# A two-layer attention and state-space kernel: scans and products of two groups in one instruction, with the preparation spread over two images

## The chip, the cores and the metric

The kernel runs on one core of one Trainium2 chip. The metric is the time of one execution in device microseconds (us). In the profile PE is TensorE's matmuls and PEld its weight loads, DVE is VectorE, ACT is ScalarE, POOL is GpSimd and SP is SyncE, whose queue issues the DMAs.

## The reference

The input is a batch of 128 images of 128 channels and 32 x 32 = 1024 pixels, fp32. The first layer is attention with four heads over the batch axis, once per pixel, with a residual and a layernorm over channels; the change doesn't touch it. The second layer has a convolution branch and a state-space branch (`_mamba`), image by image. Cut to what matters:

```python
xh = einsum('oi,bihw->bohw', cv1_w, x) + cv1_b
l = silu(batchnorm(depthwise_conv3x3(xh)))
t = layernorm(xh over channels) * ln_g + ln_b          # 1024 tokens x 128
xm, z = split(t @ in_proj_w.T)                         # 256 each
xm = silu(causal_conv1d(xm, 4 taps) + conv1d_b)
dt, Bm, Cm = split(xm @ x_proj_w.T)                    # 8, 16, 16
dt = softplus(dt @ dt_proj_w.T + dt_proj_b)
dA = exp(dt[..., None] * A)                            # 256 channels x 16 states
dBu = dt[..., None] * Bm * xm[..., None]
h = dA_t * h + dBu_t                                   # over the 1024 tokens
y = sum over states of h * C_t, plus xm * D
g = (y * silu(z)) @ out_proj_w.T
out = x + cv2(concat(l, g))
```

So each image has 256 x 16 = 4096 recurrences of 1024 steps, each with a factor (the decay dA) and an addend (the input dBu), and each result is multiplied by C and summed over the 16 states.

## The kernel before, in words

`attention_layer` writes the first layer's result to `mid` in DRAM. `mamba_layer` then takes one image per `step`.

The 4096 recurrences are cut into NG = 32 groups of 128 partitions (32 channels x 4 states); `place(k)` gives a group's half h of the channels, block nb of states and block db of channels. Per group:

- SP broadcasts dt (`dtr`) and dt times xm (`dtxr`) over the states, and B (`brep`) and C (`crep`) over the channels, from DRAM (L730, L733).
- `ahead` lets ACT compute the decay `da` (L756) and POOL the input `dbu` (L759), two groups before they are used (AHEAD).
- `group` lets DVE scan (L765) and multiply by C (L767). `da` has two buffers in PSUM, and the scan writes back into them, except in the groups of `on_pool` (6 of 32), whose scan goes to `hc` in SBUF and whose product POOL makes (`product`, L772).
- `sums` lets PE add up the states of four groups into `y_ps` (L788), and `gate` multiplies by silu(z) on DVE (L797).

While the groups of one image run, the instructions that prepare the next one (`prologue`: projections, layernorm, the 1d and 2d convolutions, dt and its product, their stores to DRAM) and those that finish the previous one (`outputs`) are issued between them. `spread` is the planner. It gives every group a slot of SLOT = 3.4 us, charges each engine what the groups use of it (`busy`), and puts each `Op`, with its cost and dependences, into the first slot where its engine has time and one of two PSUM banks is free. The order of the instructions on each engine is then fixed by the program's text: in slot k come `group(k)`, `ahead(k + 2)`, `product(k)`, loads, `sums`, `gate`, and the planned ops. The engines run their own queues in order and wait for one another.

The layernorm is four steps per half of an image: ACT centres (`centred`, L534) and squares (L537), PE averages the squares, ACT makes the reciprocal root (`rstd`, L549 and L550), POOL multiplies (`normed`, L555), and ACT applies ln_g and ln_b (`affine`, L560) into `tn`, which the four taps (`xm_mm`, L586) and z's projection (L702) read.

Images 1 to 124 run in a hardware loop, four images a pass; the others are written out before and behind it.

Of the kernel before, what the change touches and what calls it, by code (L numbers as in the profile page):

```python
# [40 lines left out]
NDB = P // GD  # L41
NG = DI2 * NNB * NDB
AHEAD = 2
# [271 lines left out]
SLOT = 3.4  # L315


def spread(ops, busy, banks, slots):
# [5 lines left out]
    for s in range(slots):  # L324
# [3 lines left out]
        while again:  # L328
            again = False
            for op in left:  # L330
# [3 lines left out]
                for d in op.deps:  # L334
                    at = max(at, ends[d] + (0.0 if d.eng == op.eng else 0.3))
# [23 lines left out]
def mamba_layer(ctx: ExitStack, tc: tile.TileContext, ident, eps, mid, w, out):  # L359
# [73 lines left out]

    wk = const.tile([P, DC, DI2 * P], F32, name="wk")
    wfT = const.tile([P, DI2, P], F32, name="wfT")
    b1c = const.tile([P, 1], F32, name="b1c")
    with tc.tile_pool(name="b_prep", bufs=1) as prep, tc.tile_pool(
# [15 lines left out]
        for h in range(DI2):  # L453
            wf_ps = prep_ps.tile([P, P], F32, name=f"wf_ps{h}")
            nc.tensor.matmul(
                wf_ps, lhsT=opw[:, h * P : (h + 1) * P], rhs=cv2gT, start=True, stop=True
            )
            nc.vector.tensor_copy(wfT[:, h, :], wf_ps)
        b_ps = prep_ps.tile([P, 1], F32, name="b_ps")
# [23 lines left out]
    dtr = several(NDB, [P, L], "dtr")  # L483
    dtxr = several(NDB, [P, L], "dtxr")
    brep = several(NNB, [P, L], "brep")
    crep = several(NNB, [P, L], "crep")
    dbu = several(4, [P, L], "dbu")
    hc = several(8, [P, L], "hc")
# [3 lines left out]
    xc = several(NCH, [P, CH], "xc")  # L492
    sq = several(NCH, [P, CH], "sq")
    dt = several(DI2, [P, L], "dt")
    sp = several(DI2, [P, L], "sp")
    o = keep.tile([P, CH], F32, name="o")
    da = several(2, [P, L], "da", psum)
    y_ps = psum.tile([P, L], F32, name="y_ps")
    banks = several(2, [P, CH], "p_ps", psum)
    xp = [t[0:NX] for t in xc]  # L500

    nc.gpsimd.memset(xpad, 0.0)
# [5 lines left out]
    def prologue(b, im):  # L508
# [9 lines left out]

        def project(wT, c):
            bank = Bank()  # L520

            def mm():
                nc.tensor.matmul(bank.tile, lhsT=wT, rhs=x[:, chunk(c)], start=True, stop=True)

            reads.append(op("PE", 0.9, mm, take=bank))
            return bank, reads[-1]

        reads, writes = [], []
        tns, xhs = [], []
        for c in range(NCH):  # L530
            bank, mm = project(w1cT, c)

            def centred(c=c, bank=bank):
                nc.scalar.activation(xc[c], bank.tile, AF.Identity, bias=b1c)  # L534
# [4 lines left out]
            e1 = op("ACT", 0.7, centred, [mm])  # L539
            e2 = op("ACT", 0.7, squared, [e1], free=bank)  # L540
# [5 lines left out]
            mm = op("PE", 0.9, variance, [e2], take=var)  # L546
# [5 lines left out]
            e3 = op("ACT", 1.4, rstd, [mm], free=var)  # L552

            def normed(c=c):
                nc.gpsimd.tensor_mul(xc[c], xc[c], sq[c])  # L555

            e4 = op("POOL", 1.4, normed, [e3])

            def affine(c=c):
                nc.scalar.activation(  # L560
                    tn[:, chunk(c, DC - 1)], xc[c], AF.Identity, bias=lnb, scale=lng
                )

            tns.append(op("ACT", 0.7, affine, [e4]))
        for c in range(NCH):
# [10 lines left out]
            xhs.append(op("ACT", 0.7, padded, [mm], free=bank))  # L576
# [3 lines left out]
        for c in range(NCH):  # L580
            for h in range(DI2):
                bank = Bank()

                def xm_mm(c=c, h=h, bank=bank):
                    for k in range(DC):
# [5 lines left out]
                            stop=k == DC - 1,  # L591
# [5 lines left out]
                late = op("PE", 3.5, xm_mm, tns[: c + 1], take=bank)  # L597
                pre.append(op("ACT", 0.6, xm_copy, [late], free=bank))
# [8 lines left out]
        silu = op("ACT", 4.9, xm_silu, pre)  # L607
# [25 lines left out]

        for h in range(DI2):
            done = []
            for c in range(NCH):
# [11 lines left out]
                def split(c=c, h=h, bank=bank):  # L648
                    bias = dtb[:, h : h + 1]
                    nc.scalar.activation(sp[h][:, chunk(c)], bank.tile, AF.Abs, bias=bias)  # L650
                    nc.scalar.activation(dt[h][:, chunk(c)], bank.tile, AF.Relu, bias=bias)  # L651

                mm = op("PE", 0.9, a_mm, [xps[c]], take=bank)
                done.append(op("ACT", 1.4, split, [mm], free=bank))

            def log1p(h=h):
                nc.scalar.activation(sp[h], sp[h], AF.Exp, scale=-1.0)
                nc.scalar.activation(sp[h], sp[h], AF.Ln, bias=1.0)  # L658

            def dt_sum(h=h):  # L660
                nc.gpsimd.tensor_add(dt[h], dt[h], sp[h])  # L661

            def dtx_mul(h=h):
                nc.gpsimd.tensor_mul(sp[h], dt[h], im["xm"][h])  # L664

            ln = op("ACT", 2.2, log1p, done)
            add = op("POOL", 2.4, dt_sum, [ln])
            op("SP", 4.0, lambda h=h: nc.sync.dma_start(im["dt"][h], dt[h]), [add])
            mul = op("POOL", 2.4, dtx_mul, [add])
            op("SP", 4.0, lambda h=h: nc.sync.dma_start(im["dtx"][h], sp[h]), [mul])  # L670
        pre = []

        for c in range(NCH):
            bank = Bank()
            last = [*xhs, late]
            for dy in range(3):
# [13 lines left out]
                if dy == 0:  # L690
                    writes += last
# [5 lines left out]
        for c in range(NCH):  # L697
            for h in range(DI2):
# [14 lines left out]
                writes.append(op("PE", 0.9, z_mm, [tns[c], late], take=bank))  # L713
                pre.append(op("ACT", 0.6, z_copy, writes[-1:], free=bank))


        def gate_silus():
            nc.scalar.activation(im["l"], im["l"], AF.Silu, bias=bnt, scale=bns)
            for h in range(DI2):
                nc.scalar.activation(im["sz"][h], im["sz"][h], AF.Silu)  # L720
            nc.scalar.preload_act_table_set("natural_log_exp_and_others")

        op("ACT", 6.0, gate_silus, pre)
        return ops, reads, writes
# [10 lines left out]
    def load_channels(im, h, db):  # L735
        rs = slice(db * GD, (db + 1) * GD)
        by_channel(dtr[db], im["dt"][h][rs])
        by_channel(dtxr[db], im["dtx"][h][rs])
# [7 lines left out]
    def place(k):  # L746
        return k // (NNB * NDB), k // NDB % NNB, k % NDB

    def on_pool(k):
        _, nb, db = place(k)  # L750
        return db == 0 and nb < NNB - 1

    def ahead(k):

        h, nb, db = place(k)
        nc.scalar.activation(  # L756
            da[k % 2], dtr[db], AF.Exp, scale=aneg[:, h * NDB + db, nb : nb + 1]
        )
        nc.gpsimd.tensor_mul(dbu[k % 4], dtxr[db], brep[nb])  # L759

    def group(k):

        h, nb, db = place(k)
        dst = hc[k % 8] if on_pool(k) else da[k % 2]
        nc.vector.tensor_tensor_scan(dst, da[k % 2], dbu[k % 4], 0.0, ALU.mult, ALU.add)  # L765
        if not on_pool(k):
            nc.vector.tensor_mul(hc[k % 8], da[k % 2], crep[nb])  # L767

    def product(k):
        if on_pool(k):  # L770
            _, nb, _ = place(k)
            nc.gpsimd.tensor_mul(hc[k % 8], hc[k % 8], crep[nb])  # L772

    def sums(im, j):
# [11 lines left out]
        for c in range(NCH):  # L786
            for db in range(NDB):
# [3 lines left out]
                    rhs=hc[(j * NDB + db) % 8][:, chunk(c)],  # L791
# [7 lines left out]
    def outputs(b, im, reads=()):  # L799


        again = Op("SP", 4.0, lambda: load_x(b), reads, first=4)
        ops = [again]
        for c in range(NCH):
# [18 lines left out]
            mm = Op("PE", 3.5, o_mm, [again], take=bank)  # L823
# [12 lines left out]
    def end(b, im):  # L836

        return {
            0: lambda: sums(im, 2 * NNB - 1),
            2: lambda: gate(im, 1),  # L840
        }

    def step(b, im, nxt, was, then=None):


        ops, reads, writes, ending = [], [], [], {}
        if nxt is not None:
            ops, reads, writes = prologue(*nxt)
        if was is not None:
            more = outputs(*was, reads)  # L850
            reads = [op for op in more if op.eng == "PE"]
            for op in writes:
                op.deps += tuple(reads)
            ops += more
            ending = end(*was)
        if then is not None:
            ops.append(Op("SP", 4.0, lambda: load_x(then), reads))
        busy = {
            "PE": [2.4 if k % 4 == 0 else 0.0 for k in range(NG)],
            "ACT": [1.15] * NG,  # L860
# [139 lines left out]
```

## Time and profile before

| | before |
|---|---|
| median of 3 runs | 17832.34 us (17829.78 to 17835.11) |
| the profiled execution's own time | 17833.07 us |
| its span | 17831.3 us |
| instructions | 183455 |
| granted TensorE clock, mean of the span | 0.884 |
| busy: PE, DVE, POOL, ACT | 78%, 87%, 75%, 61% of the span |
| first scan of the second layer starts at | 2955.24 us |
| DMA | 2242.49 MB, mean 126 GB/s |

A line of the page's groups gives the line of the code, the engine, the operation, the names of output and inputs (buffer numbers left out), their shape, the count, the busy time with the mean duration in ns, and the idle time of the engine just before such instructions with what ended most of it. The row of 40 digits shows an engine's busy share in tenths in 40 equal slices of the span, here 446 us each. In the view of waits a line is: who waited, for whom, the total in us, how often, and the longest. In the timeline it is the start, the duration, the instruction, and in brackets the idle time ahead of it.

### The profile page before, as it was taken

What the parts mean: (1) busy time and instruction counts of PE and PEld (TensorE: products, weight loads), DVE (VectorE), ACT (ScalarE), POOL (GpSimd) and SP (SyncE); (2) the same over time, 40 slices, a digit from 0 to 9 for tenths busy, and PEclk for the clock granted to TensorE, in tenths of its full rate; (3) what the DMA queues carried; (4) which work ended last, traced back from release to release, by engine and by line L of the source; (5) the groups of instructions that cost most, each with busy time, mean ns of one, the idle gap of its engine ahead of it and who ended that gap; (6) DMA issues with size and microseconds to landing.
All of it is one profiled execution on the core that took longest, in us unless ns stands there. A gap on an engine that the chain in (4) does not pass through costs nothing. (4 is left out here: it accounts for less than half of the span.)

```text
span 17831.3 us, 183455 instructions
## 1 busy us (share of the span) xinstructions
PE 13935.2 (78%) x66058; PEld 5323.4 (30%) x66058; DVE 15497.4 (87%) x10016; ACT 10805.1 (61%) x12932; POOL 13369.2 (75%) x6152
## 2 busy tenths in 40 slices
PE   9999997777777777777777777777777777777776
PEld 6666663222222222222222222222222222222221
DVE  6777776889988989998889998999998989999898
ACT  6666665556655556655556655565655565656555
POOL 1222224888888888888888888888888888888887
PEclk9999998888888888888888888888888888888888
DMA  3222222443343443343343344343334343334343
GB/s 59 49 49 47 50 39 87 145 143 137 141 144 138 144 144 136 142 144 141 140 144 138 140 144 143 139 144 140 139 143 144 138 146 143 136 141 147 140 142 122
DMA packets 1133729, 2242.49 MB, mean 126 GB/s; under 512 B 599496, under 2 KB 600528, under 8 KB 1133136
## 3 DMA queue, kind: packets, MB, share of 16 engines
q1 hardware_dynamic: 1133136, 2233.11, 37.2%
q8 instruction: 551, 9.03, 0.2%
q14 instruction: 42, 0.34, 0.0%
HBM read 1813.40 MB, written 419.43 MB: 125 GB/s over the span
## 5 line engine op out<-in xcount | busy, mean ns | idle before, releaser
L759 POOL TENSOR_TENSOR dbu<-dtxr,brep 128x1024 f32<-128x1024 f32 x4096 | 9576.6, 2363 | 1492.3 <-DMA dtxr<-dtxd 886.1
L765 DVE TENSOR_TENSOR_SCAN da<-da,dbu 128x1024 f32<-128x1024 f32 x3328 | 7610.8, 2287 | 931.7 <-ACT da L756 917.4
L756 ACT ACTIVATE da<-dtr,aneg 128x1024 f32<-128x1024 f32 x4096 | 4555.9, 1116 | 4913.7 <-DVE hc L767 4256.9
L788 PE MATMUL y_ps<-hc,fold 128*32 128x512 f32 x16384 | 3315.2, 695 | 2593.1 <-DVE hc L767 1792.3
L767 DVE TENSOR_TENSOR hc<-da,crep 128x1024 f32<-128x1024 f32 x3328 | 4073.9, 1224 | 260.1
L681 PE MATMUL p_ps<-xpad,dwd 128*128 128x512 f32 x4608 | 2432.5, 674 | 175.8 <-ACT dt L651 175.8
L788 PEld LDWEIGHTS y_ps<-hc,fold 128*32 128x32 f32 x16384 | 574.7, 117 | 5125.7 <-DVE hc L767 2779.4
L772 POOL TENSOR_TENSOR hc<-hc,crep 128x1024 f32<-128x1024 f32 x768 | 1812.8, 2360 | 328.7 <-DVE hc L765 205.5
L765 DVE TENSOR_TENSOR_SCAN hc<-da,dbu 128x1024 f32<-128x1024 f32 x768 | 1749.0, 2277 | 325.8 <-PEq L915 245.8
L242 POOL TENSOR_SCALAR yt<-z,nw,nb 128x512 f32<-128x512 f32 x256 | 319.7, 1249 | 2236.3 <-PE m_ps L176 1888.5
L586 PE MATMUL p_ps<-tn,wk 128*128 128x512 f32 x4096 | 1858.3, 601 | 126.2 <-ACT tn L560 126.1
L681 PEld LDWEIGHTS p_ps<-xpad,dwd 128*128 128x128 f32 x4608 | 927.1, 210 | 1606.4 <-issue 1323.1
L586 PEld LDWEIGHTS p_ps<-tn,wk 128*128 128x128 f32 x4096 | 745.6, 189 | 1229.4 <-issue 802.3
L640 PE MATMUL p_ps<-xc,dtwT 8*128 8x512 f32 x1024 | 582.1, 648 | 234.4 <-ACT xc L623 210.1
L614 PE MATMUL p_ps<-xm,xpT 128*40 128x512 f32 x1024 | 489.7, 601 | 283.7 <-ACT xc L623 234.9
L201 DVE TENSOR_TENSOR oT<-m_ps,rden 128x512 f32<-128x512 f32 x256 | 177.2, 692 | 587.4 <-ACT rden L200 587.4
L595 ACT COPY xm<-p_ps 128x512 f32<-128x512 f32 x512 | 299.6, 585 | 614.6 <-PE p_ps L586 614.6
L154 DVE TENSOR_TENSOR e<-s_ps,top 128x1024 f32<-128x1024 f32 x512 | 624.5, 1220 | 9.8 <-issue 1.1
L661 POOL TENSOR_TENSOR dt<-dt,sp 128x1024 f32<-128x1024 f32 x256 | 603.0, 2356 | 35.6 <-ACT sp L658 35.6
L150 DVE TENSOR_REDUCE top<-s_ps 128x8 f32<-128x1024 f32 x512 | 621.9, 1215 | 0.0
L664 POOL TENSOR_TENSOR sp<-dt,xm 128x1024 f32<-128x1024 f32 x256 | 603.9, 2359 | 0.2
L176 PE MATMUL m_ps<-ident,e 128*128 128x128 f32 x4096 | 579.0, 280 | 2.5 <-DVE v L238 1.8
(115 smaller groups left out, 16769.9 us busy)
## 6 DMA issues: line engine op xcount, KB each, us to landing
dtr<-dtd SPq DMA_DIRECT2D x1024, 512.0 KB, 4.6
dtxr<-dtxd SPq DMA_DIRECT2D x1024, 512.0 KB, 5.5
brep<-bcd SPq DMA_DIRECT2D x512, 512.0 KB, 4.7
crep<-bcd SPq DMA_DIRECT2D x512, 512.0 KB, 6.1
x<-mid SPq DMA_DIRECT2D x256, 512.0 KB, 4.2
dtd<-dt SPq DMA_DIRECT2D x256, 512.0 KB, 6.6
dtxd<-sp SPq DMA_DIRECT2D x256, 512.0 KB, 3.2
xt<-in_x SPq DMA_DIRECT2D x64, 1024.0 KB, 12.2
```

Source lines behind the costliest of these rows:

```text
L150: nc.vector.tensor_reduce(tops[half], s_ps[:, :, ls, :], AX.X, ALU.max)
L154: nc.vector.tensor_tensor(es[g % 2][:, :, ls, :], s_ps[:, :, ls, :], tops[half].unsqueeze(3).to_broadcast([P, NH, LG // 2, NB]), ALU.subtract,
L586: nc.tensor.matmul(bank.tile, lhsT=wk[:, k, h * P : (h + 1) * P], rhs=tn[:, c * CH + k : (c + 1) * CH + k], start=k == 0, stop=k == DC - 1,)
L661: nc.gpsimd.tensor_add(dt[h], dt[h], sp[h])
L664: nc.gpsimd.tensor_mul(sp[h], dt[h], im["xm"][h])
L681: nc.tensor.matmul(bank.tile.rearrange("p (r q) -> p r q", q=HH), lhsT=dwd[:, k, :], rhs=xpad[:, c * rows + dy : (c + 1) * rows + dy, dx : ...
L756: nc.scalar.activation(da[k % 2], dtr[db], AF.Exp, scale=aneg[:, h * NDB + db, nb : nb + 1])
L759: nc.gpsimd.tensor_mul(dbu[k % 4], dtxr[db], brep[nb])
L765: nc.vector.tensor_tensor_scan(dst, da[k % 2], dbu[k % 4], 0.0, ALU.mult, ALU.add)
L767: nc.vector.tensor_mul(hc[k % 8], da[k % 2], crep[nb])
L772: nc.gpsimd.tensor_mul(hc[k % 8], hc[k % 8], crep[nb])
L788: nc.tensor.matmul(y_ps[db * GD : (db + 1) * GD, chunk(c)], lhsT=fold, rhs=hc[(j * NDB + db) % 8][:, chunk(c)], start=False, stop=nb == NN ...
```

## The change

All of it is in the second layer.

- Groups go in pairs. NP = 16 pairs of two channel blocks, each a tile of 128 x 2 x 1024. One DVE scan covers 2048 elements; the first decay of the second half is set to 0 once, and ACT never writes it, so that the recurrence starts anew there. ACT still makes two decays of 1024 per pair (`decays`); POOL makes one input of 2048 (`inputs`); the product is one instruction of 2048 on DVE, or on POOL where `j % 4 == 2`.
- The scan always writes `hc` in SBUF and the product works in place in `hc`. `da` has one pair buffer in PSUM (even pairs) and one in SBUF (odd pairs). `dbu` has two pair buffers, `hc` four. `dt` and `sp` are single, `xc` is gone.
- The layernorm's ln_g is multiplied into `wk` and `inzT` once, ln_b goes into `convb`, `zb` and a correction of the first three columns (`corr`). `centred` and `affine` are gone; `normed` is a DVE instruction that reads the bank.
- `prologue` is cut in two: `first_part` (layernorm and the padded copy) of the image after next runs in the second half of a step, `second_part` of the next image in the step after it. Silus are held to slots 1 and 15 or later.
- SLOT is 3.16; the planner has a DVE op wait 3.0 us behind what it depends on.
- A pass of the loop has 12 images: images 1 to 120; 121 to 127 are written out.

```diff
@@ -39,8 +39,8 @@
 GD = 32
 NNB = DS // GN
 NDB = P // GD
+NTB = L // P
 NG = DI2 * NNB * NDB
-AHEAD = 2
...
-SLOT = 3.4
+SLOT = 3.16
+PASS = 12
+NP = NG // 2
...
-                    at = max(at, ends[d] + (0.0 if d.eng == op.eng else 0.3))
+                    wait = 0.0 if d.eng == op.eng else 3.0 if op.eng == "DVE" else 0.3
+                    at = max(at, ends[d] + wait)
...
+    corr = const.tile([P, DI2, DC - 1], F32, name="corr")
+    zb = const.tile([P, DI2], F32, name="zb")
...
+        for h in range(DI2):
+            o_ps = prep_ps.tile([P, DC + 1], F32, name=f"o_ps{h}")
+            for t in range(DC):
+                for k in range(DC - t):
+                    nc.tensor.matmul(
+                        o_ps[:, t : t + 1],
+                        lhsT=wk[:, k, h * P : (h + 1) * P],
+                        rhs=lnb,
+                        start=k == 0,
+                        stop=k == DC - t - 1,
+                    )
+            nc.tensor.matmul(
+                o_ps[:, DC : DC + 1],
+                lhsT=inzT[:, h * P : (h + 1) * P],
+                rhs=lnb,
+                start=True,
+                stop=True,
+            )
+            nc.vector.tensor_add(convb[:, h : h + 1], convb[:, h : h + 1], o_ps[:, 0:1])
+            nc.vector.tensor_scalar_mul(corr[:, h, :], o_ps[:, 1:DC], -1.0)
+            nc.vector.tensor_copy(zb[:, h : h + 1], o_ps[:, DC : DC + 1])
+        nc.vector.tensor_scalar_mul(wk, wk, lng)
+        nc.vector.tensor_scalar_mul(inzT, inzT, lng)
...
-    dtr = several(NDB, [P, L], "dtr")
-    dtxr = several(NDB, [P, L], "dtxr")
+
+    dtr = several(NDB // 2, [P, 2, L], "dtr")
+    dtxr = several(NDB // 2, [P, 2, L], "dtxr")
     brep = several(NNB, [P, L], "brep")
     crep = several(NNB, [P, L], "crep")
-    dbu = several(4, [P, L], "dbu")
-    hc = several(8, [P, L], "hc")
+    dbu = several(2, [P, 2, L], "dbu")
+    hc = several(4, [P, 2, L], "hc")
...
-    xc = several(NCH, [P, CH], "xc")
     sq = several(NCH, [P, CH], "sq")
-    dt = several(DI2, [P, L], "dt")
-    sp = several(DI2, [P, L], "sp")
+    dt = keep.tile([P, L], F32, name="dt")
+    sp = keep.tile([P, L], F32, name="sp")
     o = keep.tile([P, CH], F32, name="o")
-    da = several(2, [P, L], "da", psum)
+    da = several(1, [P, 2, L], "da_ps", psum) + several(1, [P, 2, L], "da")
     y_ps = psum.tile([P, L], F32, name="y_ps")
     banks = several(2, [P, CH], "p_ps", psum)
-    xp = [t[0:NX] for t in xc]
...
+    xp = several(NCH, [NX, CH], "xp")
+
+    for t in da:
+        nc.vector.memset(t[:, 1, 0:1], 0.0)
...
-    def prologue(b, im):
+    def first_part(im, after=(), start=0):
...
+            e1 = op("ACT", 0.7, squared, [mm])
             var = Bank()
 
             def variance(c=c, bank=var):
                 nc.tensor.matmul(bank.tile, lhsT=mean, rhs=sq[c], start=True, stop=True)
 
-            mm = op("PE", 0.9, variance, [e2], take=var)
+            mm = op("PE", 0.9, variance, [e1], take=var)
 
             def rstd(c=c, bank=var):
                 nc.scalar.activation(sq[c], bank.tile, AF.Ln, bias=eps)
                 nc.scalar.activation(sq[c], sq[c], AF.Exp, scale=-0.5)
 
-            e3 = op("ACT", 1.4, rstd, [mm], free=var)
-
-            def normed(c=c):
-                nc.gpsimd.tensor_mul(xc[c], xc[c], sq[c])
-
-            e4 = op("POOL", 1.4, normed, [e3])
-
-            def affine(c=c):
-                nc.scalar.activation(
-                    tn[:, chunk(c, DC - 1)], xc[c], AF.Identity, bias=lnb, scale=lng
+            e2 = op("ACT", 1.4, rstd, [mm], free=var)
+
+            def normed(c=c, bank=bank):
+                nc.vector.scalar_tensor_tensor(
+                    tn[:, chunk(c, DC - 1)], bank.tile, b1c, sq[c], ALU.add, ALU.mult
                 )
 
-            tns.append(op("ACT", 0.7, affine, [e4]))
+            tns.append(op("DVE", 0.75, normed, [e2], free=bank))
...
+    def second_part(im, written=(), silus=(0, 0)):
...
-                            stop=k == DC - 1,
+                            stop=c > 0 and k == DC - 1,
+                        )
+                    if c == 0:
+                        nc.tensor.matmul(
+                            bank.tile[:, 0 : DC - 1],
+                            lhsT=ident,
+                            rhs=corr[:, h, :],
+                            start=False,
+                            stop=True,
                         )
...
-    def place(k):
-        return k // (NNB * NDB), k // NDB % NNB, k % NDB
-
-    def on_pool(k):
-        _, nb, db = place(k)
-        return db == 0 and nb < NNB - 1
-
-    def ahead(k):
-
-        h, nb, db = place(k)
-        nc.scalar.activation(
-            da[k % 2], dtr[db], AF.Exp, scale=aneg[:, h * NDB + db, nb : nb + 1]
+    def place(j):
+
+        return j // (2 * NNB), j // 2 % NNB, j % 2
+
+    def on_pool(j):
+        return j % 4 == 2
+
+    def both(t):
+
+        return t.unsqueeze(1).to_broadcast([P, 2, L])
+
+    def flat(t):
+        return t.rearrange("p k l -> p (k l)")
+
+    def decays(j):
+
+
+        h, nb, q = place(j)
+        for i in range(2):
+            k = h * NDB + 2 * q + i
+            nc.scalar.activation(
+                da[j % 2][:, i, i:], dtr[q][:, i, i:], AF.Exp, scale=aneg[:, k, nb : nb + 1]
+            )
+
+    def inputs(j):
+        _, nb, q = place(j)
+        nc.gpsimd.tensor_mul(dbu[j % 2], dtxr[q], both(brep[nb]))
+
+    def scan(j):
+
+        nc.vector.tensor_tensor_scan(
+            flat(hc[j % 4]), flat(da[j % 2]), flat(dbu[j % 2]), 0.0, ALU.mult, ALU.add
         )
-        nc.gpsimd.tensor_mul(dbu[k % 4], dtxr[db], brep[nb])
-
-    def group(k):
-
-        h, nb, db = place(k)
-        dst = hc[k % 8] if on_pool(k) else da[k % 2]
-        nc.vector.tensor_tensor_scan(dst, da[k % 2], dbu[k % 4], 0.0, ALU.mult, ALU.add)
-        if not on_pool(k):
-            nc.vector.tensor_mul(hc[k % 8], da[k % 2], crep[nb])
-
-    def product(k):
-        if on_pool(k):
-            _, nb, _ = place(k)
-            nc.gpsimd.tensor_mul(hc[k % 8], hc[k % 8], crep[nb])
+
+    def product(j):
+        _, nb, _ = place(j)
+        eng = nc.gpsimd if on_pool(j) else nc.vector
+        eng.tensor_mul(hc[j % 4], hc[j % 4], both(crep[nb]))
...
-                    rhs=hc[(j * NDB + db) % 8][:, chunk(c)],
+                    rhs=hc[(2 * j + db // 2) % 4][:, db % 2, chunk(c)],
...
-        again = Op("SP", 4.0, lambda: load_x(b), reads, first=4)
+    def outputs(b, im):
+
+        again = Op("SP", 4.0, lambda: load_x(b), first=1)
...
-            0: lambda: sums(im, 2 * NNB - 1),
-            2: lambda: gate(im, 1),
+            1: lambda: sums(im, 2 * NNB - 1),
+            3: lambda: gate(im, 1),
...
+    SILUS = (1, 15)
+
+    def step(b, im, nxt=None, was=None, then=None):
...
+        if was is not None:
+            ops += outputs(*was)
+            ending = end(was[1])
+        xs = [op for op in ops if op.eng == "PE"]
         if nxt is not None:
-            ops, reads, writes = prologue(*nxt)
-        if was is not None:
-            more = outputs(*was, reads)
-            reads = [op for op in more if op.eng == "PE"]
-            for op in writes:
-                op.deps += tuple(reads)
+            more, reads = second_part(nxt, xs, SILUS)
             ops += more
-            ending = end(*was)
         if then is not None:
-            ops.append(Op("SP", 4.0, lambda: load_x(then), reads))
+            ops.append(Op("SP", 4.0, lambda: load_x(then), xs))
+            reads.append(ops[-1])
+            ops += first_part(im, reads, NG // 2 + 2)
...
-            "PE": [2.4 if k % 4 == 0 else 0.0 for k in range(NG)],
-            "ACT": [1.15] * NG,
-            "POOL": [4.8 if on_pool(k) else 2.4 for k in range(NG)],
+            "PE": [2.4 if k % 4 == 1 else 0.0 for k in range(NG)],
+            "ACT": [0.0, 2.3] * (NG // 2),
+            "POOL": [k % 2 * 4.5 * (1 + on_pool(k // 2)) for k in range(NG)],
...
-                group(k)
-                a = k + AHEAD
-                if a < NG:
-                    ahead(a)
-                elif nxt is not None:
-                    ahead(a - NG)
-                product(k)
-                h, nb, db = place(a % NG)
-                if nb == NNB - 1 and a < NG:
-                    if h == 0:
-                        load_channels(im, 1, db)
-                    elif nxt is not None:
-                        load_channels(nxt[1], 0, db)
-                if nxt is not None:
-                    if k == 25:
-                        load_b(nxt[1], 0)
-                        load_c(nxt[1], 0)
-                    if k == 30:
-                        load_b(nxt[1], 1)
-                    if k == 31:
-                        load_c(nxt[1], 1)
-                if k in (2, 6):
-                    load_b(im, 2 + k // 4)
-                if k in (3, 7):
-                    load_c(im, 2 + k // 4)
+                j = k // 2
+                if k % 2 == 0:
+                    scan(j)
+                else:
+                    a = j + 2
+                    h, nb, q = place(a % NP)
+                    src = im if a < NP else nxt
+                    if src is not None:
+                        decays(a % NP)
+                        inputs(a % NP)
+                        if nb == NNB - 1 and (h == 0 or nxt is not None):
+                            for do in load_dt, load_dtx:
+                                for db in 2 * q, 2 * q + 1:
+                                    do(im if h == 0 else nxt, 1 - h, db)
+                    product(j)
+                for src, do, slots in (
+                    (im, load_b, {1: 3}),
+                    (im, load_c, {3: 2, 5: 3}),
+                    (nxt, load_b, {18: 0, 21: 1, 24: 2}),
+                    (nxt, load_c, {22: 0, 30: 1}),
+                ):
+                    if k in slots and src is not None:
+                        do(src, slots[k])
+                if k % 4 == 1 and k > 1:
+                    sums(im, k // 4 - 1)
                 if k in ending:
                     ending[k]()
-                if k % NDB == 0 and k > 0:
-                    sums(im, k // NDB - 1)
-                if k == NG // 2 + 2:
+                if k == NG // 2 + 3:
...
-    step(0, a, (1, b), None, 2)
-    with tc.For_i(1, NB - 3, 4) as i:
-        for j in range(0, 4, 2):
-            step(i + j, b, (i + j + 1, a), (i + j - 1, a), i + j + 2)
-            step(i + j + 1, a, (i + j + 2, b), (i + j, b), i + j + 3)
+    step(0, a, b, None, 2)
+    with tc.For_i(1, NB - 7, PASS) as i:
+        for j in range(0, PASS, 2):
+            step(i + j, b, a, (i + j - 1, a), i + j + 2)
+            step(i + j + 1, a, b, (i + j, b), i + j + 3)
...
```

## The prediction

> **What bounds the kernel now.** I read the page's busy shares and 40 slices first, then its groups of instructions.
>
> ```profile
> PE 13935.2 (78%) x66058; PEld 5323.4 (30%) x66058; DVE 15497.4 (87%) x10016; ACT 10805.1 (61%) x12932; POOL 13369.2 (75%) x6152
> ...
> DVE  6777776889988989998889998999998989999898
> ...
> POOL 1222224888888888888888888888888888888887
> ...
> L759 POOL TENSOR_TENSOR dbu<-dtxr,brep 128x1024 f32<-128x1024 f32 x4096 | 9576.6, 2363 | 1492.3 <-DMA dtxr<-dtxd 886.1
> L765 DVE TENSOR_TENSOR_SCAN da<-da,dbu 128x1024 f32<-128x1024 f32 x3328 | 7610.8, 2287 | 931.7 <-ACT da L756 917.4
> ...
> L767 DVE TENSOR_TENSOR hc<-da,crep 128x1024 f32<-128x1024 f32 x3328 | 4073.9, 1224 | 260.1
> ```
>
> The 75% and 87% of the first line mix two stages. From slice 7 on the second layer runs, with POOL at 8 tenths and DVE at 8 to 9: DVE sets its pace and POOL has little to spare. Next I asked what DVE waited for between 4000 and 17700 us, some 118 images.
>
> ```profile
> DVE da L765 <- ACT da L756: 844.4, 385, 4.3
> DVE hc L765 <- PEq L915: 238.2, 29, 9.6
> DVE da L765 <- POOL dbu L759: 12.3, 3, 4.6
> ```
>
> Per image that is 7.2 us for ScalarE's decays (which stand behind table loads and silus in its queue), 2.0 us for the loop's end, which comes once in four images, and almost nothing for POOL. Last, in order of time, DVE and POOL side by side:
>
> ```profile
> 10066.04 2.27 DVE L765 TENSOR_TENSOR_SCAN da<-da,dbu 128x1024 f32<-128x1024 f32 x1
> 10066.25 2.36 POOL L772 TENSOR_TENSOR hc<-hc,crep 128x1024 f32<-128x1024 f32 x1 [0.83 <-issue]
> 10068.34 1.23 DVE L767 TENSOR_TENSOR hc<-da,crep 128x1024 f32<-128x1024 f32 x1
> 10068.56 4.68 POOL L759 TENSOR_TENSOR dbu<-dtxr,brep 128x1024 f32<-128x1024 f32 x2
> ```
>
> The engines overlap at full speed. The code shows what these DVE instructions share: da lies in PSUM, so every scan and product of the kernel before reads one operand from PSUM and only one from SBUF. The sole large exception is a multiplication in the preparation, during which POOL is idle:
>
> ```profile
> L446 DVE TENSOR_TENSOR wk<-wk,inxT 128x1024 f32<-128x1024 f32 x1 | 1.2, 1226 | 4.2 <-DMA wk<-in_conv1d_wT 4.2
> ```
>
> Two SBUF operands cost DVE nothing by themselves (1226 against 1224 ns). Beside a working POOL this trace never shows them.
>
> **The time to start from.** The profiled execution took 17833.07 us, its span 17831.3; the median shown is 17832.34, so the three are interchangeable. The first scan starts at 2955.24 (timeline); from there, 14876 us / 128 = 116.2 us per image. The first layer is untouched. So new time = 17831.3 + 128 x (new us per image - 116.2).
>
> [...] The trace has 1272 ns for 512 (L555) and 2363 for 1024: 1091 per 512, hence 4545 for 2048[...].
>
> **The change, part by part.** Durations of the double instructions: a product is 692 ns at 512 (L201) and 1224 at 1024, so 532 per 512 and a fixed 160; at 2048 it is 2.29 us. A scan is 2 x 2287 - 160 = 4.41 us.
>
> 1. *Pairs.* Per image 32 scans become 16 and 26 products on DVE become 12. Starts, not durations, add up: today scan to product 2.30 to 2.39 and product to next scan 1.14. DVE before: 26 x 3.49 + 6 x 2.2 + two gates at 1.13 = 106.2; with the waits above 115.4, near 116.2. DVE after: 16 x 4.46 + 12 x 2.20 + 2.3, and two new normed instructions at 0.7 = 101.4. So at full speed the pairs save 4.8 us, most of it since one product in four, not 6 in 32, goes to POOL.
> 2. *POOL.* 20 instructions at 4.50 = 90.0 (16 inputs, 4 products) and four of dt and dtx at 2.36 = 9.4: 99.4 us. Before: 38 x 2.36 + 9.4 + 2.5 of normed = 101.6.
> 3. *Where operands lie.* The scan now writes hc in SBUF, and the product reads hc and crep: two SBUF operands in all 12. The da of odd pairs is in SBUF, and dbu too: 8 scans of 16. That is 8 x 4.41 + 12 x 2.29 = 62.8 us of DVE work[...]. Before, it was zero. This part decides. Its price lies between nothing and full exclusion; I take full exclusion[...] and the trace shows why the case did not arise.
> 4. *Decays.* Freed by the scan of two pairs earlier, they have one scan and up to two products (4.4 + 2.3 + 2.3 = 9.0 us) for 2.2 us of work, enough for a silu group (two loads at 1.28 and two activations at 1.1: 4.8 us). The 7.2 us of waits should go; what is late next is POOL's inputs, which have the same 9.0 us for 4.5, or for 9.0 where a product stands in front of them.
> 5. *Layernorm folded.* ScalarE loses 2 x 0.68 + 2 x 0.80 = 3.0 us, POOL 2.5, DVE gains 1.4 (in item 1), PE gets two matmuls of three columns (0.3 us at most each, in PE's free 22%). Setup gets some 20 small matmuls, about 10 us once. Nothing here is on the path except DVE's 1.4.
> 6. *Preparation over two images.* The same instructions and the same DMAs move (per image 8 dt, 8 dtx, 8 b and c, 2 x, 4 stores), on queues with room: SP's transfers take 40% of the DMA engines. They land in 4 to 7 us and are issued two pairs, some 13 us, before use; before, POOL waited 814 us in all for dtxr. I price this at 0, and at 2 us per image if they come late. The new DVE wait, normed on ScalarE's rstd, has the next scan queued behind it; the planner puts it 3 us late. 0 to 1 us.
> 7. *Twelve images a pass.* 31 loop ends become 10: from 238/118 = 2.0 us per image to about 0.8; I use 1.0.
>
> **The sum for full exclusion.** [...]99.4 + 62.8 = 162.2 us per image; the 8 scans from PSUM (35.3 us), gates and normed hide beside POOL. Going through four pairs: a locked scan waits for POOL's inputs, POOL's next inputs wait until that scan frees one of two dbu buffers[...]. With the loop 1.0: 165.2, or 17831 + 128 x 49.0 = 24100 us. Between 160.5 (starts a little closer than durations: 23500) and 170 (0.1 us for each of some 40 hand-overs: 24700).
>
> **The rivals.**
> *Sharing without a lock.* [...]2048 x 1.04 ns = 2.13 us, for 20 instructions 42.6; with POOL's 99.4 it makes 142, or 21300 us. If only the products contend (a scan needs its operands half as fast), 99.4 + 27.5 + 1 = 128: 19300 us.[...]
> *No contention: faster.* If DVE's second SBUF read is not in POOL's way at all, DVE sets the pace with 101.4, POOL at 99.4 is nearly as long and two dbu buffers tie them closely, for which I add 4 to 5 us; with the loop 107 us, or 16650 (16150 at 102.5 without any coupling, 17200 at 111). For it: nothing in the trace has been seen to contend. Against: the trace holds no test[...]. It decides below a quarter: once more than 116.2 - 1 - 99.4 = 15.8 of the 62.8 us exclude POOL, the gain is gone.
> *No effect within 0.2%* (36 us, about what a measurement of this kernel tells from no change) needs gain and contention to cancel to 0.3 us per image.
>
> **Chances.** Full exclusion 0.42, partial 0.16, none 0.39, cancelling 0.02, otherwise slower 0.01. Likeliest is 24100, by itself 23400 to 24700. Since "none" holds more than 2 in 10, the range runs from 16250 to 24700. Faster 0.39, same 0.02, slower 0.59.
>
> **What would show it.** Right: in the second layer POOL and DVE busy times that no longer overlap for L-lines of products and odd scans; products well over 2.29 us, or starting only as POOL's inputs end; odd scans slower or later than even ones of the same size; per image near 165 us. Wrong: odd and even scans both at 4.4 us, products at 2.3 beside a POOL at 4.5, and DVE busy over 95% of each slice. A step between 125 and 145 us points to sharing. Waits of DVE for ScalarE's decays should be near zero in all cases; if they remain, item 4 is wrong.

## The result, and the profile after

| | before | after |
|---|---|---|
| median | 17833.17 us (17829.78 to 17835.11, 4 runs) | 23335.07 us (23334.36 to 23335.38, 4 runs) |
| span of the profiled execution | 17831.3 us | 23333.6 us |
| first scan of the second layer | 2955.24 us | 2977.31 us |
| per image from there (span less first scan, / 128) | 116.2 us | 159.0 us |
| busy DVE, POOL | 87%, 75% | 95%, 84% |

The ratio is 1.3085, 95% interval 1.3063 to 1.3108: slower by 31%. The first layer is as it was. The page of the changed kernel, the same parts as were shown of before:

```profile
PE 14726.9 (63%) x66614; PEld 5612.4 (24%) x66614; DVE 22202.8 (95%) x6442; ACT 10518.5 (45%) x12420; POOL 19500.3 (84%) x3592
...
DVE  7777689999999999999999999999999999999999
...
POOL 1222189999999999999999999999999999999998
...
L819 POOL TENSOR_TENSOR dbu<-dtxr,brep 128x2048 f32<-128x2048 f32 x2048 | 13687.0, 6693 | 1440.2 <-DVE hc L823 1284.7
L830 DVE TENSOR_TENSOR hc<-hc,crep 128x2048 f32<-128x2048 f32 x1536 | 8463.9, 5510 | 52.9
L823 DVE TENSOR_TENSOR_SCAN hc<-da,dbu 128x2048 f32<-128x2048 f32 x1024 | 6828.8, 6669 | 25.3 <-POOL dbu L819 17.7
...
L823 DVE TENSOR_TENSOR_SCAN hc<-da_ps,dbu 128x2048 f32<-128x2048 f32 x1024 | 4514.9, 4409 | 153.9 <-PEq L981 134.6
```

DVE issues 36% fewer instructions and is busy for 43% longer. The last two lines are the same instruction of the same size, in equal number: with the decays in PSUM (`da_ps`, even pairs) it takes 4409 ns, with the decays in SBUF (`da`, odd pairs) 6669. The product takes 5510 ns where 2.29 us were expected, POOL's input 6693 where 4.50 were. And DVE almost never waits, by the view of its waits from 4000 us to 23200:

```profile
DVE hc L823 <- PEq L981: 134.6, 9, 15.0
DVE hc L823 <- issue: 13.9, 1, 13.9
DVE hc L823 <- POOL dbu L819: 8.8, 1, 8.8
```

The 7 us per image of waits for decays are gone, as planned, and no other wait of DVE has taken their place. (POOL waits 1197 us in the same stretch for scans to free its buffers.) DVE's time is inside its instructions. The timeline of DVE and POOL (start, duration) shows how:

```profile
9995.85 4.39 DVE L823 TENSOR_TENSOR_SCAN hc<-da,dbu 128x2048 f32<-128x2048 f32 x1
9996.00 8.56 POOL L819 TENSOR_TENSOR dbu<-dtxr,brep 128x2048 f32<-128x2048 f32 x1 [1.18 <-DVE hc L823]
10000.27 6.44 DVE L830 TENSOR_TENSOR hc<-hc,crep 128x2048 f32<-128x2048 f32 x1
...
10004.52 6.56 POOL L830 TENSOR_TENSOR hc<-hc,crep 128x2048 f32<-128x2048 f32 x1
10006.64 4.41 DVE L823 TENSOR_TENSOR_SCAN hc<-da_ps,dbu 128x2048 f32<-128x2048 f32 x1
...
10011.05 11.04 POOL L819 TENSOR_TENSOR dbu<-dtxr,brep 128x2048 f32<-128x2048 f32 x2
10011.08 6.66 DVE L830 TENSOR_TENSOR hc<-hc,crep 128x2048 f32<-128x2048 f32 x1
```

The odd scan comes first and runs at its own 4.39 us. POOL's input, issued 0.15 us later, ends after 8.56: it stood still until the scan was nearly over, and ended 4.3 us after it. The product, issued meanwhile, ends 2.2 us after that input, POOL's product 4.4 us after the DVE product. In these lines one of the two engines stands while DVE has an instruction with two SBUF inputs and POOL a multiplication; only the scan from PSUM (10006.64, 4.41 us) runs beside POOL undisturbed. The last two lines start together (x2: two instructions in one line).

From such lines one gets how long each keeps the other out. The product of the last line ends after 6.66 us, so the POOL input kept it out for 6.66 - 2.29 = 4.4 us. POOL's own instruction is 4.53 us where nothing is in its way, so the scan at 9995.85 kept it out for 4.2 us from its start (0.15 + 8.56 - 4.53), and products, in other such lines, for 2.15. In the trace of the second layer there are 1028 meetings of these three kinds in which the first instruction runs at its own length and the second starts within 1 us of it. In all of them the second is blocked, each kind for nearly the same time (4.36 to 4.42, 4.20 to 4.27, 2.15 to 2.19 us). Per image 20 x 4.4 (16 inputs, and 4 products of the same size) + 4 x 2.2 (dt and dtx) + 8 x 4.2 + 12 x 2.15 = 156 us, of 159.0 measured. I call this sum the held time. Laid along the trace from 4000 to 22000 us, it leaves some 3 us per image in which nobody holds anything, which makes up the rest.

### The profile page after: what moved, and what is told of

Read it like the earlier page. It is cut to its first block, busy times and chain, and to the rows that moved or that the text cites. A ratio compares the mean times of both kernels' runs of the same rounds, so it can differ in the third digit from the quotient of the medians.

```text
span 23333.6 us, 172625 instructions
## 1 busy us (share of the span) xinstructions
PE 14726.9 (63%) x66614; PEld 5612.4 (24%) x66614; DVE 22202.8 (95%) x6442; ACT 10518.5 (45%) x12420; POOL 19500.3 (84%) x3592
## 5 line engine op out<-in xcount | busy, mean ns | idle before, releaser
L819 POOL TENSOR_TENSOR dbu<-dtxr,brep 128x2048 f32<-128x2048 f32 x2048 | 13687.0, 6693 | 1440.2 <-DVE hc L823 1284.7
L830 DVE TENSOR_TENSOR hc<-hc,crep 128x2048 f32<-128x2048 f32 x1536 | 8463.9, 5510 | 52.9
L823 DVE TENSOR_TENSOR_SCAN hc<-da,dbu 128x2048 f32<-128x2048 f32 x1024 | 6828.8, 6669 | 25.3 <-POOL dbu L819 17.7
L813 ACT ACTIVATE da<-dtr,aneg 128x1024 f32<-128x1024 f32 (+1 forms) x2048 | 2239.6, 1141 | 5794.2 <-DVE hc L823 5792.4
L823 DVE TENSOR_TENSOR_SCAN hc<-da_ps,dbu 128x2048 f32<-128x2048 f32 x1024 | 4514.9, 4409 | 153.9 <-PEq L981 134.6
L813 ACT ACTIVATE da_ps<-dtr,aneg 128x1024 f32<-128x1024 f32 (+1 forms) x2048 | 2287.8, 1117 | 3101.3 <-DVE hc L823 3051.6
L846 PE MATMUL y_ps<-hc,fold 128*32 128x512 f32 x16384 | 2662.3, 779 | 1352.0 <-POOL hc L830 1314.6
L830 POOL TENSOR_TENSOR hc<-hc,crep 128x2048 f32<-128x2048 f32 x512 | 3361.4, 6565 | 0.0
L682 PE MATMUL p_ps<-xp,dtwT 8*128 8x512 f32 x1024 | 750.5, 821 | 863.4 <-ACT dt L693 768.6
L837 PE MATMUL y_ps<-xm,skipd 128*128 128x512 f32 x1024 | 783.1, 908 | 110.0 <-DVE sz L855 110.0
```

What stands on the lines that cost most here:

```text
L682: nc.tensor.matmul(bank.tile, lhsT=dtwT[XD:NX, h * P : (h + 1) * P], rhs=xp[c][XD:NX], start=True, stop=True,)
L813: nc.scalar.activation(da[j % 2][:, i, i:], dtr[q][:, i, i:], AF.Exp, scale=aneg[:, k, nb : nb + 1])
L819: nc.gpsimd.tensor_mul(dbu[j % 2], dtxr[q], both(brep[nb]))
L823: nc.vector.tensor_tensor_scan(flat(hc[j % 4]), flat(da[j % 2]), flat(dbu[j % 2]), 0.0, ALU.mult, ALU.add)
L830: eng.tensor_mul(hc[j % 4], hc[j % 4], both(crep[nb]))
L837: nc.tensor.matmul(y_ps[:, chunk(c)], lhsT=skipd[:, h, :], rhs=im["xm"][h][:, chunk(c)], start=True, stop=False,)
```

## The experiments

The theory: a DVE instruction with two SBUF operands and a reading POOL instruction exclude each other, whole instruction against whole instruction, and the held time is the bound. The rivals: operands in SBUF are slow by themselves; the pairs, with two input buffers, couple the engines too closely; the folded layernorm and the spread preparation cost the time. Runs given below without a ratio were timed once.

**POOL only writes.** The inputs are left out of the computation; POOL fills their buffer instead.

```diff
-        nc.gpsimd.tensor_mul(dbu[j % 2], dtxr[q], both(brep[nb]))
+        nc.gpsimd.memset(dbu[j % 2], 0.5)
+        nc.gpsimd.memset(dbu[j % 2], 0.25)
+        nc.gpsimd.memset(dbu[j % 2][:, 0, :], 0.5)
```

> The changed kernel, with POOL's 16 input products per image replaced by three memsets into the same buffer (2048, 2048 and 1024 elements), so that POOL is about as long at work but only writes there; the inputs are left out of the computation. Exclusion of POOL's reads: only POOL's 4 products and 4 dt and dtx instructions per image still read, 27 us, against 62.8 us of DVE instructions with two SBUF operands; DVE sets the pace with about 101 us plus at most 4 x 4.4 us, so 103 to 118 us per image, 16200 to 18100 us in all, odd scans mostly at 4.4 us and products mostly at 2.3 us. Rival 'SBUF operands are slow by themselves': products stay at 5.5 us and odd scans at 6.7 us in the mean, total above 22500. Rival 'two input buffers couple the engines too closely': the order and the buffers are unchanged, so the total stays above 21000.

Measured: 18283 us, 119.6 us per image. The groups of instructions:

```profile
L825 DVE TENSOR_TENSOR_SCAN hc<-da,dbu 128x2048 f32<-128x2048 f32 x1024 | 5040.8, 4923 | 1662.7 <-POOL dbu L821 1617.1 <-PE y_ps L848 29.8 <-PE p_ps L570 9.4
...
L832 DVE TENSOR_TENSOR hc<-hc,crep 128x2048 f32<-128x2048 f32 x1536 | 3524.3, 2294 | 52.6
L832 POOL TENSOR_TENSOR hc<-hc,crep 128x2048 f32<-128x2048 f32 x512 | 3245.7, 6339 | 2.0 <-DVE hc L825 2.0
```

The product with the same operands in SBUF is back at 2294 ns: SBUF operands aren't slow by themselves, that rival falls. POOL writes for 4.6 us per pair beside it (memsets of 1804, 1804 and 951 ns), and neither is lengthened. But the total is a little above my upper end of 18100: DVE now waits for POOL's buffers (1617 us in all, 12.6 us per image). That is the coupling, and it is looked at below.

**Four products per image from PSUM.**

```diff
-            flat(hc[j % 4]), flat(da[j % 2]), flat(dbu[j % 2]), 0.0, ALU.mult, ALU.add
+            flat(da[0] if j % 4 == 0 else hc[j % 4]),
+            flat(da[j % 2]),
+            flat(dbu[j % 2]),
...
-        eng.tensor_mul(hc[j % 4], hc[j % 4], both(crep[nb]))
+        src = da[0] if j % 4 == 0 else hc[j % 4]
+        eng.tensor_mul(hc[j % 4], src, both(crep[nb]))
...
```

These products stand ahead of the decays, and a memset of one column restores the 0 at the seam.

> The changed kernel, but the four scans per image with j % 4 == 0 write back into the PSUM buffer, so that their four products on DVE read one operand from PSUM; the decays that follow wait for the product. Exclusion: the held time falls by 4 x 2.29 = 9.2 us per image, from 159 to about 150, so 22150 us (21900 to 22500), these four products at 2.3 us and the other eight and the odd scans still lengthened. 'Slow by themselves': the four products fall from 5.5 to 2.3 us, 13 us per image less, about 21700. 'Coupling': no gain or a loss, since the decays wait longer: 23300 or more.

Measured: 22294 us, ratio to before 1.2511 (1.2475 to 1.2547), 150.9 us per image: 8.1 us less than the changed kernel, where the held time is 8.6 to 9.2 less. The two kinds of product in one kernel:

```profile
L836 DVE TENSOR_TENSOR hc<-hc,crep 128x2048 f32<-128x2048 f32 x1024 | 5192.9, 5071 | 35.1
...
L836 DVE TENSOR_TENSOR hc<-da_ps,crep 128x2048 f32<-128x2048 f32 x512 | 1173.3, 2292 | 49.6
```

Both write `hc` in SBUF; only one input has moved, and 5071 ns become 2292. It is the inputs that count here.

**The kernel before, with decays in SBUF.** First a control, two input buffers in place of four, which makes room in SBUF for the decays (the indices `k % 4` become `k % 2`).

```diff
-    dbu = several(4, [P, L], "dbu")
+    dbu = several(2, [P, L], "dbu")
...
```

> The kernel before with two buffers of inputs in place of four: the control for the next run. POOL may run only two groups ahead. All theories: DVE operands are unchanged, so at most some waits of DVE for POOL appear: 17830 to 18600 us, scans at 2.29 us and products at 1.22 us.

Measured: 17895 us, 116.7 us per image, scans at 2290 ns and products at 1224. Then, on top of it, the place alone:

```diff
-    da = several(2, [P, L], "da", psum)
+    da = several(2, [P, L], "da")
```

> The control with the decay buffers moved from PSUM to SBUF and nothing else: single groups, four images a pass, the old preparation. Now all 32 scans and 26 products per image have two SBUF operands. Exclusion of whole instructions: POOL's 100 us and DVE's 32 x 2.29 + 26 x 1.22 = 105 us can't overlap, 200 to 206 us per image, 28500 to 29400 us in all. Sharing read by read: 100 + 58 x 1024 x 1.04 ns = 162 us, 23700. Only products contend: 100 + 32 = 132 us, 19900. If the pairing or the new order were the cause and not the place of the operands: as the control, below 18600.

Measured: 27855 us, 194.5 us per image, 56% over the control for one word less in a line. This has no pairs, no new order, none of the rest. It lies under my 200 to 206, which added durations; the held times (half of those above) give 42 x 2.2 + 2 x 1.1 + 32 x 2.1 + 26 x 1.07 = 190. Sharing read by read (162) and contention of products alone (132) are out. In the timeline two instructions issued 0.03 us apart:

```profile
14997.66 2.34 POOL L759 TENSOR_TENSOR dbu<-dtxr,brep 128x1024 f32<-128x1024 f32 x1 [2.23 <-DVE da L765]
14997.69 3.40 DVE L767 TENSOR_TENSOR hc<-da,crep 128x1024 f32<-128x1024 f32 x1
15001.00 2.28 DVE L765 TENSOR_TENSOR_SCAN da<-da,dbu 128x1024 f32<-128x1024 f32 x1
```

POOL, first, loses nothing (2.34 us); the product takes 1.23 + 2.17.

**More work for the busiest engine.** All products of the changed kernel go to DVE:

```diff
-        return j % 4 == 2
+        return False
```

> The changed kernel with all 16 products per image on DVE, none on POOL. DVE is the engine that is busy 95% of the span, so by busy shares this adds four products to the bottleneck: at their mean of 5.5 us that is 22 us per image more, 26150 us, or at their bare 2.29 us 9 us more, 24500. Exclusion says the opposite: [...]the held time falls by 4 x 2.2 = 8.7 us to about 150 us per image: 22200 us (21900 to 22500).

Measured: 22830 us, ratio 1.2806 (1.278 to 1.2831): 505 us faster than the changed kernel. The direction is the theory's, against what the busy shares say. The size is under half, and the time above my 22500: 155.1 us per image is 3.9 less, where the held time of 147 is 9 less (4.4 us less 2.15 for each product that moves). POOL now waits 36 us per image (4637 us in all) for scans to free its buffers, and for some of that nobody holds anything:

```profile
15060.19 8.71 DVE L823 TENSOR_TENSOR_SCAN hc<-da,dbu 128x2048 f32<-128x2048 f32 x1
15068.83 4.39 DVE L823 TENSOR_TENSOR_SCAN hc<-da_ps,dbu 128x2048 f32<-128x2048 f32 x1
...
15073.30 13.01 POOL L819 TENSOR_TENSOR dbu<-dtxr,brep 128x2048 f32<-128x2048 f32 x2 [8.68 <-DVE hc L823]
```

While the scan from PSUM of the second line runs, POOL has no free buffer to write. Laid along this trace (4000 to 16000 us), the held times leave about 8 us per image in which nobody holds anything, 5.5 of them during scans from PSUM; in the changed kernel it was 3. These 5 us are the missing half.

**No reading product on POOL either.** As the first run, and POOL's products are memsets too.

```diff
-        eng.tensor_mul(hc[j % 4], hc[j % 4], both(crep[nb]))
+        if on_pool(j):
+            fill(hc[j % 4])
+        else:
+            nc.vector.tensor_mul(hc[j % 4], hc[j % 4], both(crep[nb]))
...
```

`fill` stands for the three memsets of the first run.

> As the run with memsets for POOL's inputs, but POOL's four products per image are three memsets into hc too, so that of POOL only the four dt and dtx instructions per image still read; inputs and these products are left out of the computation. It shows what pairs would give with almost no exclusion. If the prediction's rival of no contention was sized rightly: 107 us per image, 16650 us, odd scans at 4.4 to 4.6 us. If two input buffers of pairs couple DVE and POOL more than that, it stays near the 119.6 us per image of the run that left POOL's products reading: 18000 to 18300 us, with DVE waiting for POOL.

Measured: 17910 us, 116.6 us per image. Only dt and dtx still read, and the scans that meet one can be picked out of the timeline:

```profile
8223.14 2.36 POOL L706 TENSOR_TENSOR sp<-dt,xm 128x1024 f32<-128x1024 f32 x1
8223.22 6.57 DVE L828 TENSOR_TENSOR_SCAN hc<-da,dbu 128x2048 f32<-128x2048 f32 x1 [7.50 <-POOL dbu L810]
...
8237.49 4.40 DVE L828 TENSOR_TENSOR_SCAN hc<-da,dbu 128x2048 f32<-128x2048 f32 x1
8237.64 1.81 POOL L808 MEMSET dbu<- 128x2048 f32 x1 [3.11 <-DVE hc L828]
```

Behind a reading POOL instruction, with which it shares no tile, the scan takes 6.57 us, beside a memset 4.40. So the exclusion is worth at least 159.0 - 116.6 = 42 us per image. It also shows how little the pairs would gain without it. DVE still waits for POOL's buffers,

```profile
DVE hc L828 <- POOL dbu L810: 1022.1, 481, 7.5
```

for 10 us per image (4000 to 16000 us, some 103 images), while POOL waits 13 us per image for scans to free them (1369 us): each by turns, with two buffers as the only reserve. Two things make this run too slow as a picture of pairs without exclusion: two scans per image still stand behind dt or dtx (2 x 2.15 us), and three memsets take 4.67 us with their gaps where an input takes 4.53 (20 x 0.14). By this estimate at most 7.1 us may be taken off, which leaves 109.5 to 116.6, against 116.2 before.

**The rest of the change, without pairs.** First the loop alone, in the kernel before:

```diff
-    with tc.For_i(1, NB - 3, 4) as i:
-        for j in range(0, 4, 2):
+    with tc.For_i(1, NB - 7, 12) as i:
+        for j in range(0, 12, 2):
...
```

> The kernel before with twelve images a pass of the loop in place of four, and nothing else. DVE waits 8.2 us at a loop's end, 31 times before and 10 times here: 21 x 8.2 to 12 us, so 17580 to 17660 us.[...]

Measured: 17683.07 us, ratio 0.992 (0.9903 to 0.9936): 139 us less, somewhat under the expected 172 to 250. DVE's waits at loop ends fell by 171 us (245.8 to 74.8, 8.3 us for each of 9 ends seen), and its waits for decays rose by 22. Then all of the change but pairs and places:

```diff
-    da = several(1, [P, 2, L], "da_ps", psum) + several(1, [P, 2, L], "da")
+    da = several(2, [P, L], "da", psum)
...
+        dst = hc[k % 8] if on_pool(k) else da[k % 2]
+        nc.vector.tensor_tensor_scan(dst, da[k % 2], dbu[k % 4], 0.0, ALU.mult, ALU.add)
...
```

> The changed kernel's layernorm folded into weights, preparation over two images and twelve images a pass, but single groups with the decays in PSUM and the old order of scans and products. No instruction of DVE has two SBUF operands in the loop. Exclusion: nothing is lengthened; DVE needs 106.2 + 1.4 us, the loop 0.8, and the 7 us of waits for decays may stay or shrink: 109 to 116 us per image, 16900 to 17800 us, so the loss of the change is all in pairs and places. If the spread preparation or the folded layernorm cost much of the change's 43 us per image: above 19000.

Measured: 17611.97 us, ratio 0.9882 (0.9865 to 0.9898). Folded layernorm and spread preparation are 71 us better than the loop alone; they cost nothing, so that rival falls too. Then with more products on POOL:

```diff
-        return db == 0 and nb < NNB - 1
+        return db == 0
```

> The same with eight products per image on POOL in place of six: DVE 2 x 1.29 = 2.6 us shorter per image (105 us), POOL 2 x 2.33 longer (102 us). If DVE sets the pace: about 250 us less than the version with six. If POOL is by now as late as DVE: no gain or a loss of up to 300 us.

Measured: 17164.36 us, ratio 0.9632 (0.9616 to 0.9648), 448 us less than with six where 250 were expected. The busy time of DVE's scans and products falls by 323 us (13433 to 13110), near the 2.6 x 128 = 333 reckoned for them, and the idle time ahead of its scans, products and normed instructions by 116 (1114 to 997), 58 of it waits for POOL's inputs. And ten:

```diff
-        return db == 0
+        return db == 0 or db == 2 and nb == 1
```

> Single groups with decays in PSUM, folded layernorm, spread preparation and twelve images a pass, now with ten products per image on POOL in place of eight. DVE another 2.6 us shorter (102 us), POOL 4.7 longer (106 us). If DVE and its waits for decays still set the pace: 16850 to 17000. If POOL is now the later of the two: 17164 or more.

Measured: 17036.65 us, ratio 0.9556 (0.954 to 0.9572), between the two expectations: 109.8 us per image. POOL has become about as late as DVE; its products wait 345 us in all, after 1053 with eight. This version beats both kernels. Its scans and products, with POOL at work for some 106 of 110 us (46 instructions at 2.31 from start to start, the median step in the trace of before), are at their bare durations:

```profile
L810 DVE TENSOR_TENSOR_SCAN da<-da,dbu 128x1024 f32<-128x1024 f32 x2816 | 6431.5, 2284 | 156.9 <-ACT da L801 154.6 <-POOL dbu L804 1.4
L812 DVE TENSOR_TENSOR hc<-da,crep 128x1024 f32<-128x1024 f32 x2816 | 3446.8, 1224 | 222.3 <-PE p_ps L653 0.5 <-DVE da L810 0.5
```

## Why the prediction was right, point by point

The forecast of 24100 us missed the measured 23335 by 3%; 23335 lies just below the likeliest case's own 23400 to 24700 and inside the range. The case that was forecast, full exclusion, is what happened. The range, 16250 to 24700, also held the rival of no contention, so that lying in it says little. And full exclusion had a chance of 0.42 against 0.39 for none: no line of the trace before could tell them apart, and the choice between them was my estimate.

- *Item 3, the place of operands.* Shown. Moving the decays to SBUF in the kernel before costs 78 us per image; removing POOL's reads from the changed kernel gives 42 back. The first to start keeps the other out until it is nearly over: a POOL input of 4.53 us for 4.4, an odd scan of 4.41 for 4.2, a DVE product of 2.29 for 2.15. With the decays in SBUF, too, the second is blocked in the full (3.40 for 1.23 us), not by halves; memsets block nothing (products at 2294 ns).
- *The sum.* 165.2 us per image was forecast, 159.0 measured. The mis-sized term: durations in place of held times (162.2 against 156). The 3 us added to the durations, 2 for time in which neither engine keeps the other out and 1 for the loop's end, were about right: some 3 us per image are free in the trace. The bound "starts a little closer than durations", 160.5, was the better reckoning.
- *Items 1 and 2.* The bare durations were right: scans 4409 ns for 4.41, products 2291 at the least for 2.29, POOL 4.53 for 4.50. (The 4.50 was my estimate; 1272 and 2363 ns for 512 and 1024 elements give 4.55.)
- *Item 4.* Right: DVE's waits for decays in the loop went from 844 us to none. That didn't matter, as DVE itself was so late. *Item 5:* the first scan starts 22 us later (2977.31 for 2955.24), where about 10 us were reckoned for the setup; the matmuls of three columns take 0.17 to 0.25 us each, for at most 0.3. *Item 6:* POOL's waits for dtxr fell from 814 to 96 us in the views from 4000 us on; the preparation costs nothing. *Item 7:* 9 loop ends cost DVE 134.6 us, 1.1 us per image, for 1.0; one end takes 15 us, after 8.2 (238.2 / 29) before.
- *The rival of no contention* was priced too low. I gave it 107 us per image, with 4 to 5 us for the coupling of DVE and POOL through two buffers. The run with memsets in place of nearly all POOL reads puts it between 110 and 117, so the coupling costs 7 to 14 us. (A slip in that paragraph: 102.5 us per image makes 16080 us, not 16150.) *The rival of sharing* falls with the decays in SBUF: 194.5 us per image, where it gave 162.
- *What would show it.* I expected busy times that "no longer overlap". The trace counts a blocked instruction as busy (POOL's input at 9996.00 with 8.56 us for 4.53), so both engines look busy at once: 95% and 84%. For the same reason DVE at over 95% of each slice, which I had put down as a sign of being wrong, came true here (4940 to 4955 us busy of each 5000). The lengthened durations were the right sign. Of DVE's 159 us per image only some 101 are its own work.

What stays open is whether it is POOL's reading alone that counts: memsets differ from its multiplications in more than that, and a POOL instruction with one input was not tried. By the held times, the instruction that starts first in the trace also goes first, in all but 9 of 5593 in the changed kernel; in those 9 the two start within 0.02 us of each other, and which of them goes first is not explained.

## What to carry to other kernels

Where VectorE and GpSimd both work all the time, count for each VectorE instruction how many of its inputs lie in SBUF. With two of them, it and a GpSimd instruction that read two inputs ran one after the other in each of the 1028 meetings counted here. The bound was then the held time of both engines together, 156 of 159.0 us per image, and not the longer engine. One input in PSUM was worth more here than halving the number of instructions: single groups with it, and ten products on POOL, came to 109.8 us per image, pairs to 159.0, and pairs nearly without exclusion to 110 to 117. And an engine at 95% busy may be standing: compare the mean duration of one instruction with the shortest of its group (5510 and 2291 ns for the product here) before moving work away from it.

## What had not been expected of the hardware

Taking products from POOL and giving them to the busiest engine made the kernel 505 us faster, as a product adds 4.4 us to the held time on POOL (in the timeline above it ends 4.4 us after the DVE product that blocked it) and 2.15 on DVE. Memsets on POOL, 1.80 us for 2048 elements, run beside DVE instructions with two SBUF operands and lengthen nothing (products 2292 ns, an odd scan 4.40 us). And the clock granted to TensorE was lower in the slow kernels, at less PE work per time (PE busy 78% before, 63% after): 0.884 before, 0.775 after, 0.747 with all decays in SBUF, 0.891 in the fastest version. It doesn't follow the time strictly: single groups with six products on POOL ran 17612 us at 0.870. It isn't the cause: DVE's scan of a pair from PSUM takes 4.41 us at 0.775, and 4.41 at 0.844 where POOL mostly writes. Why it falls was not tried.
